# The end of an adaLN and routed-FFN kernel: column steps behind the last product, stores on two queues, and the bias load behind the gathers

## The chip, the cores and the metric

The kernel runs on one core of one Trainium2 chip. A core has five engines that work side by side and are held together by semaphores: TensorE (PE in the profile; its weight loads have their own row, PEld), VectorE (DVE), ScalarE (ACT), GpSimd (POOL) and SyncE (SP). Each engine takes its instructions in the order in which they stand in its queue. Transfers between HBM and on-chip memory are issued from SP, ACT or POOL and carried out by 16 DMA engines that all of these share. The metric is the device time of one execution in microseconds. Lower is better. Three runs of the kernel before took 415.0, 415.74 and 415.83 us, median 415.74.

## What is computed

All numbers are float32. x has 64 batches of 64 rows and 1,024 columns.

```python
W = weights[condition]                       # per batch a 64x64 matrix, chosen by an index 0..15
c = einsum('bct,bcd->bdt', x, W)
logits = c @ gate_w.T + expert_bias          # 4 experts
one_hot = one_hot(argmax(logits))
base  = einsum('bth,oh->bto', c, W_up)       # 1024 x 1024
z     = einsum('nh,erh->ner', c, lora_A)     # 4 experts, rank 8
delta = einsum('ner,ehr->neh', z, lora_B)    # taken for the chosen expert alone
out = x + base + delta
```

So each batch is mixed along its rows by a chosen 64x64 matrix and multiplied by one wide matrix that all batches share.

## The kernel before

The kernel swaps the two products. It first multiplies x by one matrix that holds the gate (4 columns), lora_A (32 columns) and W_up (1,024 columns), 1,060 columns in all; the result is called u. Then it applies the 64x64 matrices to u. Two batches make a **pair** of 128 rows, so there are 32 pairs, and two pairs, called a and b, make a **group**. The matrix is cut in halves along both axes, into blocks B11, B12, B21 and B22 of 512 x 530; each pair's x into two halves of 512 columns (A11 and A12 for pair a, A21 and A22 for pair b).

To keep float32 accuracy, every operand is split into a high part, rounded to fp32r by ScalarE (`ah`, `hB`, `uh` in the profile), and a low part, the rest, taken by VectorE (`al`, `lB`, `ul`). A product is three matmuls: high by high, high by low, low by high. The first two groups take eight block products each (`eight`). All later groups take seven, from sums and differences of blocks (`seven`): `S1` to `S4` of x, and the blocks `T1` to `T4`.

**From u to the output.** The columns of a pair's u are worked off in column steps. `finish(i, j)` is one step: `apply` (three matmuls of the 64x64 matrices, laid out as one 128x128 block `bd`, with `uh`, `uh`, `ul`), `delta` (one matmul that adds the chosen expert's part, from `zt`), and `evict`, which moves the result out of PSUM. The first step of a pair holds the 36 gate and lora columns; `gate` (six small VectorE operations, the first of which, `lg`, adds `bias_sb`) finds the expert and makes `z`, and `turn` transposes it by TensorE and splits it into `zt`. For most pairs `evict` copies to `y`, POOL adds x by an accumulating transfer, and SP stores. For the last pair (`i == NP - 1`, pair b of the last group), and for the last two steps of pair a, x has been loaded into `y` before; VectorE adds, and a store of that step follows at once. The first 480 columns of pair a are stored by themselves.

**The order of work** is written out by hand. `InOrder` wraps the five engines and keeps each one's instructions in the order in which the program makes them. A product runs over four rows `k` of a block, and `hooks` name what is put in after which row. All these calls go through one helper, so they carry line 43 in the profile and are told apart by their tiles.

**The start.** TensorE runs `WARM` small matmuls on a tile of zeros while the first loads come in (`keep_warm`, line 385). Then the first group's products begin with A11 and A21 by B11, row by row. The loads stand on SP's queue in the order B11 row 0, B11 row 1, rest of the first half of x for both pairs, B11 rows 2 and 3, the second half of x (`xx`, one transfer for A12 and A22), B21, B12. After row 0 come the hooks of line 519 on: five more small matmuls, the split of row 1, `make_idx` (a matmul and a VectorE operation that turn the conditions into row indices) and four `load_cond`, gathers of 64x64 matrices that POOL issues by these indices. POOL's queue before them holds constants and, in line 473, the load of the bias, repeated over 128 partitions.

**The end.** In the last group the last wide product, S4 by B22, is made by `product_by_bank`: its 530 columns lie in two PSUM banks, 258 and 272 columns, one worked off after the other. `u_bank(m)` adds the earlier sum `t8` and makes the high part of bank m's u for pair a; `u_bank_low(m)` makes its low part. The column steps of pair b stand between and within the banks, those of pair a behind.

Of the kernel before, what the change touches and what calls it, by code (L numbers as in the profile page):

```python
# [15 lines left out]
P = 128  # L16
# [3 lines left out]
E, R = 4, 8  # L20
# [6 lines left out]

COLS = ((0, 356), (356, 352), (708, 352))
LAST = ((0, 356), (356, NB - 356), (NB, 258), (NB + 258, NB - 258))
WARM = 28  # L30
GATE = (("lg", E), ("mx", 1), ("sc", E), ("m2", 1), ("zm", ER))
HALVES = (slice(0, 64), slice(64, 128))

# [13 lines left out]
def kernel(  # L47
# [147 lines left out]
    def chain():  # L195
        return psum.tile([P, 1024], F32, name="c", tag="c", bufs=3)
# [47 lines left out]
    def u_low(i, n, src):  # L244
        h, lo = us[i]
        vector.tensor_sub(lo[:, n], src, h[:, n].bitcast(F32))
# [5 lines left out]
    def half(hf):  # L252
        return slice(NB * hf, NB * hf + NB)
# [101 lines left out]
    def evict(i, j):  # L355

        s, d = ycols(i, j)
        o = os_.pop((i, j))[:, s]
        if i == NP - 1 or d.start >= FIRST and i == NP - 2:
            vector.tensor_add(ys[i][:, d], o, ys[i][:, d])  # L360
            if d.start == FIRST:
                d = slice(STORED, d.stop)
            sync.dma_start(out[i, :, d], ys[i][:, d])
            return
        if i < NP - 2 and j == 0:
            ys[i] = yp.tile([P, H], F32, name="y", tag="y")
        scalar.copy(ys[i][:, d], o)
        if i == NP - 2 and j == 1:
            n = slice(0, FIRST)
            pool.dma_start(ys[i][:, n], x[i][:, n], accum_op=ALU.add)  # L370
        elif j == 2:
            pool.dma_start(ys[i], x[i], accum_op=ALU.add)
            nc.sync.dma_start(out[i], ys.pop(i))

    def finish(i, j, o=None):
        apply(i, j, o)
        delta(i, j)
        evict(i, j)
# [91 lines left out]
    for e in range(E):  # L470
        pool.memset(rank[:, e : e + 1], float(E - e))
    bias_sb = cpool.tile([P, E], F32, name="bias_sb")
    pool.dma_start(bias_sb, bias.to_broadcast([P, E]))
    b3 = cpool.tile([3 * ER, H], F32R, name="b3")

    PARTS = slice(0, COLS[0][1] - G), slice(COLS[0][1] - G, H)
# [28 lines left out]
    def eight(g):  # L505
        a, b = 2 * g, 2 * g + 1
        h = [[] for _ in range(6 if g == 0 else 8)]

        def at(s, k, fn, *args):
            h[s].append((k, fn, *args))  # L510

        def each(s, k, fn, q, ks, *args):
            for i in ks:
                at(s, k, fn, q, i, *args)

        one, two = (0, 1), (2, 3)
        if g == 0:
            each(0, -1, load_b, "B12", range(KH))
            at(0, 0, keep_warm, 5)
            for n in pieces:  # L520
                at(0, 0, split_b, "B11", 1, n)
            at(0, 0, make_idx)
            for i in range(4):
                at(0, 0, load_cond, i)
            at(0, 0, split_a, g, "A11", STEPS[2])
            each(0, 0, split_b, "B11", (2,))
            at(0, 0, split_a, g, "A21", STEPS[2])
            each(0, 0, split_b, "B11", (3,))
            at(0, 0, split_a, g, "A12")
            each(0, 0, split_b, "B21", (0,))  # L530
            at(0, 1, split_a, g, "A22")
            each(0, 2, split_b, "B21", (1, 2))
            each(0, 3, split_b, "B21", (3,))
            each(1, -1, load_b, "B22", range(KH))
            at(1, 0, load_b3)
            for i in (2, 3):
                at(1, 0, load_half, i, 0)
            each(1, 0, split_b, "B12", (0,))
            each(1, 1, split_b, "B12", (1,))
            each(1, 2, split_b, "B12", two)  # L540
            at(1, 2, split_cond, a)
            at(1, 3, split_cond, b)
            each(1, 3, split_b, "B22", (0,))
            at(2, -1, lambda: u_of(a, 0, c["1"]))
            at(2, 0, load_two, 0)
            at(2, 0, load_two, 1)
            each(2, 0, split_b, "B22", (1,))
            at(2, 2, apply, a, 0)
            at(2, 2, gate, a)
            at(2, 2, lambda: u_of(b, 0, c["2"]))  # L550
            at(2, 3, split_b3, PARTS[0])
            at(3, 1, turn, a)
            for i in (2, 3):
                at(3, 0, load_half, i, 1)
            each(3, 1, split_b, "B22", two)
            at(3, 2, split_a, g + 1, "A11")
            at(3, 3, delta, a, 0)
            at(3, 3, evict, a, 0)
            at(3, 3, split_b3, PARTS[1])
            at(4, 1, apply, b, 0)  # L560
            at(4, 1, gate, b)
            at(4, 2, split_a, g + 1, "A21")
            at(5, -1, lambda: u_of(a, 1, c["3"]))
            at(5, 0, turn, b)
            at(5, 0, sum_t1, one)
            at(5, 0, load_two, 2)
            at(5, 0, load_two, 3)
            at(5, 2, delta, b, 0)
            at(5, 2, evict, b, 0)
            at(5, 2, end_t1, one)  # L570
            at(5, 3, split_a, g + 1, "A12")
            at(5, 3, finish, a, 1)
            order = (
                [("1", "A11", "B11", True), ("2", "A21", "B11", True)],
                [("1", "A12", "B21", False), ("2", "A22", "B21", False)],
                ("3", "A11", "B12", True),
                ("1", "A21", "B12", True),
                ("3", "A12", "B22", False),
                ("1", "A22", "B22", False),
            )  # L580
        else:
            p = a - 1
            at(0, -1, lambda: u_of(p, 1, cs[g - 1]["1"]))
            at(0, 1, finish, p - 1, 2)
            at(0, 1, split_a, g, "A22")
            at(0, 2, make_t1, two)
            at(0, 3, finish, p, 1)
            at(1, 0, finish, p, 2)
            at(1, 1, load_cond, a + 2)
            at(1, 1, load_cond, b + 2)  # L590
            for i in (b + 2, a + 2):
                at(1, 1, load_half, i, 0)
                at(2, 1, load_half, i, 1)
            at(2, 1, make_t2, one)
            at(3, -1, lambda: u_of(a, 1, c["1"]))
            at(3, 2, make_t2, two)
            at(4, -1, lambda: u_of(b, 1, c["2"]))
            at(4, 1, sums, g + 1, "S1")
            at(4, 2, split_cond, a)
            at(4, 2, split_cond, b)  # L600
            at(5, 0, sums, g + 1, "S2")
            at(5, 1, split_a, g + 1, "A11")
            at(5, 2, sums, g + 1, "S3")
            at(6, 0, split_a, g + 1, "S2")
            at(7, -1, lambda: u_of(a, 0, c["3"]))
            at(7, 0, sums, g + 1, "S4")
            order = (
                ("1", "A11", "B12", True),
                ("2", "A21", "B12", True),
                ("1", "A12", "B22", False),  # L610
                ("2", "A22", "B22", False),
                ("3", "A11", "B11", True),
                ("1", "A21", "B11", True),
                ("3", "A12", "B21", False),
                ("1", "A22", "B21", False),
            )
        run(g, order, h, c)
        cs[g] = dict(c)


    def seven(g):
# [123 lines left out]
        if last:  # L745

            z = chain()
            turn(b, z[:, :512])
            u_add(b, c["3"], ts["t7"])
            scalar.copy(us[b][0][:, half(1)], ts["u", b])  # L750
            keep_sum("t8", c["3"], "t6")
            u_low(b, half(1), ts["u", b])
            s = temp("usum")
            places = place(), place()

            def u_bank(m):
                n = LAST_BANKS[m]
                vector.tensor_add(s[:, n], places[m][:, : n.stop - n.start], ts["t8"][:, n])
                scalar.copy(us[a][0][:, NB + n.start : NB + n.stop], s[:, n])

            def u_bank_low(m):
                n = LAST_BANKS[m]
                u_low(a, slice(NB + n.start, NB + n.stop), s[:, n])

            product_by_bank(
                g,
                places,
                "S4",
                "B22",
                [  # L770
                    (3, lambda: finish(b, 0, z[:, 512:])),
                    (3, u_bank, 0),
                    (5, lambda: finish(b, 1, chain()[:, :512])),
                    (5, u_bank_low, 0),
                ],
            )
            sync.dma_start(out[a, :, :STORED], ys[a][:, :STORED])
            u_bank(1)
            finish(b, 2, chain()[:, :512])
            u_bank_low(1)  # L780
            finish(a, 2)
            finish(a, 3)

# [49 lines left out]
```

## Time and profile before

| what | value |
|---|---|
| three runs | 415.0, 415.74, 415.83 us |
| the profiled execution, its own time | 415.6 us |
| its span, first to last instruction | 413.8 us |
| PE busy | 409.4 us, 99% of the span |
| DVE, ACT, POOL busy | 286.2, 185.1, 74.9 us |
| granted TensorE clock | 0.999 of full speed |
| start of the first product | 4.18 us |
| bias load issued on POOL's queue | 4.20 us |
| end of the last matmul | 410.46 us |
| last store issued on SP's queue | 410.96 us |

The profile is of one execution. Its span leaves out 1.8 us of the execution's own time that lie outside the first and last instruction. A row of the timeline gives start, duration, engine, line, operation, the tiles written and read (`out<-in`), their shapes, and in brackets the idle time before it with what ended it. `xN` merges N instructions that follow each other. The ends of matmuls are modelled and overlap the next ones, so it is their starts that are to be compared. In the table of waits a row reads: who waited, for whom, us in total, how often, longest. In the DMA view a queue's row gives packets, megabytes and the share of 16 engines' time in that window; q1 is SP's queue, q10 ACT's, q0 POOL's.

### The profile page before, as it was taken

How to read it: one execution, taken by the hardware profiler on the slowest of the kernel's cores; microseconds unless marked ns; L12 is line 12 of the kernel's file. 1: busy time of each engine (PE TensorE's matmuls, PEld its weight loads, DVE VectorE, ACT ScalarE, POOL GpSimd, SP SyncE). 2: the span in 40 equal slices, each digit the busy share in tenths (PEclk: the TensorE clock that was granted, in tenths of full speed). 3: DMA queues.
4: the chain of work that ended last, by engine and by line, in shares of the span. 5: the costliest groups of instructions: out<-in, count | busy, mean ns of one | idle time of the engine just before them, and what ended most of it. 6: DMA issues, size and time to landing. Idle time of an engine off the chain costs nothing.

```text
span 413.8 us, 8162 instructions
## 1 busy us (share of the span) xinstructions
PE 409.4 (99%) x3193; PEld 407.9 (99%) x3193; DVE 286.2 (69%) x648; ACT 185.1 (45%) x419; POOL 74.9 (18%) x92
## 2 busy tenths in 40 slices
PE   9999999999999999999999999999999999999996
PEld 8999999999999999999999999999999999999996
DVE  5887786866767666676676767666676676766766
ACT  5846744453534445333353534445333343533531
POOL 5205412020020201102020020201102020020000
PEclk9999999999999999999999999999999999999999
DMA  8989974543656435465452556434465442555345
GB/s 266 314 288 229 242 175 87 148 121 98 174 133 169 98 89 144 128 177 125 111 124 95 171 135 174 104 84 139 126 179 135 107 122 93 170 140 149 52 101 178
DMA packets 25830, 60.99 MB, mean 147 GB/s; under 512 B 3328, under 2 KB 5344, under 8 KB 25792
## 3 DMA queue, kind: packets, MB, share of 16 engines
q1 hardware_dynamic: 18544, 41.00, 27.9%
q0 software_dynamic: 6704, 19.21, 27.1%
q8 instruction: 25, 0.41, 0.4%
q10 hardware_dynamic: 544, 0.26, 0.2%
q14 instruction: 13, 0.11, 0.1%
HBM read 43.68 MB, written 16.78 MB: 146 GB/s over the span
## 4 chain that ended last, share of the span: by engine, by line
PE 99%; DVE 0%; issue 0%
PE c L43 82%; PE o L43 17%; DVE y L43 0%; DVE warm L43 0%; DVE one L43 0%
## 5 line engine op out<-in xcount | busy, mean ns | idle before, releaser
L43 PE MATMUL c<-hT,ah 128*128 128x264 f32 x480 | 139.7, 291 | 0.0
L43 PE MATMUL c<-lT,ah 128*128 128x264 f32 x480 | 137.3, 286 | 0.0
L43 PE MATMUL c<-hT,al 128*128 128x264 f32 x480 | 137.1, 286 | 0.0
L43 PE MATMUL c<-hB,ah 128*128 128x264 f32 (+1 forms) x424 | 121.8, 289 | 0.0
L43 PE MATMUL c<-hB,al 128*128 128x264 f32 (+1 forms) x424 | 121.2, 287 | 0.0
L43 PE MATMUL c<-lB,ah 128*128 128x264 f32 (+1 forms) x424 | 119.1, 287 | 0.0
L43 PEld LDWEIGHTS c<-lT,ah 128*128 128x128 f32 x480 | 91.0, 190 | 0.0
L43 PEld LDWEIGHTS c<-hT,ah 128*128 128x128 f32 x480 | 90.9, 189 | 0.0
L43 PEld LDWEIGHTS c<-hT,al 128*128 128x128 f32 x480 | 90.7, 189 | 0.0
L43 POOL DMA_DIRECT2D y<-in_x_dram x31 | 29.7, 957 | 289.6 <-ACT y L43 284.5
L43 PEld LDWEIGHTS c<-hB,ah 128*128 128x128 f32 x424 | 80.8, 190 | 0.3 <-issue 0.3
L43 PEld LDWEIGHTS c<-hB,al 128*128 128x128 f32 x424 | 80.7, 190 | 0.2 <-issue 0.2
L43 PEld LDWEIGHTS c<-lB,ah 128*128 128x128 f32 x424 | 79.6, 190 | 0.1
L43 ACT COPY y<-o 128x352 f32<-128x352 f32 (+1 forms) x91 | 40.1, 443 | 58.2 <-PE o L43 55.1
L43 ACT CAST uh<-usum 128x530 fp32r<-128x530 f32 (+4 forms) x44 | 27.1, 616 | 69.7 <-DVE usum L43 69.7
L43 DVE TENSOR_TENSOR al<-S,ah 128x512 fp32r<-128x512 f32 x56 | 38.5, 688 | 24.1 <-ACT ah L43 24.1
L43 DVE TENSOR_TENSOR al<-xh,ah 128x512 fp32r<-128x512 f32 x46 | 31.7, 690 | 29.9 <-ACT ah L43 29.9
L43 PE MATMUL o<-uh,bd 128*128 128x356 f32 (+2 forms) x186 | 44.8, 322 | 0.0
L43 DVE TENSOR_TENSOR ul<-usum,uh 128x530 fp32r<-128x530 f32 (+4 forms) x44 | 30.1, 683 | 18.7 <-ACT uh L43 18.6
L43 ACT CAST zt<-o 96x128 fp32r<-96x128 f32 x31 | 8.1, 262 | 76.4 <-PE o L43 76.4
L43 POOL DMA_INDIRECT wsel<-in_cw_dram,idx x32 | 34.2, 1070 | 11.9 <-issue 5.2
L43 ACT CAST ah<-S 128x512 fp32r<-128x512 f32 x56 | 34.9, 623 | 1.8 <-DVE S L43 1.4
(88 smaller groups left out, 472.2 us busy)
## 6 DMA issues: line engine op xcount, KB each, us to landing
xh<-in_xt_dram SPq DMA_DIRECT2D x60, 256.0 KB
y<-in_x_dram POOLq DMA_DIRECT2D x30, 512.0 KB, 5.6
out_dram<-y SPq DMA_DIRECT2D x30, 512.0 KB
wraw<-in_w_dram SPq DMA_DIRECT2D x23, 265.0 KB
T<-in_w_dram POOLq DMA_DIRECT2D x8, 265.0 KB, 7.8
xx<-in_xt_dram SPq DMA_DIRECT2D x1, 512.0 KB
wsel<-in_cw_dram,idx POOLq DMA_INDIRECT x32, 5.0
y<-in_x_dram SPq DMA_DIRECT2D x1, 512.0 KB
```

What stands on the lines that cost most here:

```text
L43: return lambda *a, **k: self.tc.keep_in_program_order(fn(*a, **k))
```

## The change

It has four parts. `WARM` goes from 28 to 30, and the small matmuls after the first row from 5 to 1. The bias load moves on POOL's queue from ahead of the gathers to behind them. The last product keeps its two banks, but no column step stands within it: all three of pair b follow behind bank 1, and the VectorE operations are reordered to that, with the low part of b's second half behind the sum of bank 0. The three stores of the last pair are issued by ScalarE, not SP.

```diff
-WARM = 28
+WARM = 30
@@ def evict(i, j, o=None)
             if d.start == FIRST:
                 d = slice(STORED, d.stop)
-            sync.dma_start(out[i, :, d], ys[i][:, d])
+            queue = scalar if i == NP - 1 else sync
+            queue.dma_start(out[i, :, d], ys[i][:, d])
             return
@@ constants
     bias_sb = cpool.tile([P, E], F32, name="bias_sb")
-    pool.dma_start(bias_sb, bias.to_broadcast([P, E]))
@@ def eight(g), g == 0
-            at(0, 0, keep_warm, 5)
+            at(0, 0, keep_warm, 1)
             for n in pieces:
                 at(0, 0, split_b, "B11", 1, n)
             at(0, 0, make_idx)
             for i in range(4):
                 at(0, 0, load_cond, i)
+            at(0, 0, lambda: pool.dma_start(bias_sb, bias.to_broadcast([P, E])))
@@ def seven(g), last group
             keep_sum("t8", c["3"], "t6")
-            u_low(b, half(1), ts["u", b])
@@
                 "S4",
                 "B22",
-                [
-                    (3, lambda: finish(b, 0, z[:, 512:])),
-                    (3, u_bank, 0),
-                    (5, lambda: finish(b, 1, chain()[:, :512])),
-                    (5, u_bank_low, 0),
-                ],
+                [(3, u_bank, 0), (3, lambda: u_low(b, half(1), ts["u", b]))],
             )
+            u_bank(1)
+            u_bank_low(0)
+            finish(b, 0, z[:, 512:])
+            u_bank_low(1)
+            finish(b, 1, chain()[:, :512])
             sync.dma_start(out[a, :, :STORED], ys[a][:, :STORED])
-            u_bank(1)
             finish(b, 2, chain()[:, :512])
-            u_bank_low(1)
             finish(a, 2)
             finish(a, 3)
```

## The prediction

> **What bounds the kernel now.** I read the page first: busy shares and the chain that ended last.
>
> ```profile
> PE 409.4 (99%) x3193; PEld 407.9 (99%) x3193; DVE 286.2 (69%) x648; ACT 185.1 (45%) x419; POOL 74.9 (18%) x92
> PE 99%; DVE 0%; issue 0%
> ```
>
> TensorE is never off the chain until the last eviction, so time can only be won where TensorE stands still, does work that is not needed, or after it has ended. I took the step from each matmul's start to the next in the timeline and compared it with the usual step of its shape (0.123 us for 264 columns, 0.126 for 272, 0.16 for 352). Between 13.5 and 409.4 us just one place is late (62.1 us, 0.2 us, behind TensorE's own earlier results). So three places are left: the start up to 13.5 us, the last two column steps, and the time after the last matmul. TensorE at the start, then what feeds it:
>
> ```profile
> 7.01 0.47 PE L43 MATMUL o<-warm 128*128 128x128 bf16 x5
> 7.41 0.18 PE L43 MATMUL o<-condf,batch 2*128 2x32 bf16 x1
> 7.53 0.39 PE L43 MATMUL c<-hB,ah 128*128 128x264 f32 x1
> ...
> 12.59 0.51 PE L43 MATMUL c<-lB,ah 128*128 128x264 f32 x2
> 12.94 0.28 PE L43 MATMUL c<-hB,ah 128*128 128x264 f32 x1
> 13.19 0.39 PE L43 MATMUL c<-hB,al 128*128 128x264 f32 x1
> ```
> ```profile
> 10.34 0.62 ACT L43 CAST ah<-xx 128x512 fp32r<-128x512 f32 x1 [1.36 <-DMA xx<-in_xt_dram]
> 11.16 0.64 ACT L43 CAST hB<-wraw 128x530 fp32r<-128x530 f32 x1 [0.19 <-issue]
> 11.70 0.61 ACT L43 CAST ah<-xx 128x512 fp32r<-128x512 f32 x1
> ```
> ```profile
> 11.82 0.71 DVE L43 TENSOR_TENSOR lB<-wraw,hB 128x530 fp32r<-128x530 f32 x1
> 12.45 0.69 DVE L43 TENSOR_TENSOR al<-xx,ah 128x512 fp32r<-128x512 f32 x1
> ```
>
> The low part of B21's row 0 ends at 12.53 and TensorE's `lB` matmul starts at 12.59; the low part of A22 ends at 13.14 and TensorE's `al` matmul starts at 13.19. Two waits, and behind each a weight load that nothing hides. By the starts (12.441, 12.591, 12.817, 12.941, 13.192, 13.420) the steps are 0.150, 0.226, 0.251 and 0.228 against about 0.124: 0.36 us lost. Both chains begin at 10.34, when ScalarE had waited 1.36 us for x's second half. Why it lands so late is in the DMA view of 9.10 to 10.25 us:
>
> ```profile
> q1 hardware_dynamic: 204, 0.38, 92.7%
> q0 software_dynamic: 5, 0.00, 9.3%
> ```
>
> Five packets with no bytes to speak of took 9.3% of 16 engines for 1.15 us, 1.7 us. By the packet records two 128-byte packets of POOL's queue took 0.84 us each (9.12 to 9.96, 9.36 to 10.20); the only transfer on that queue by then, apart from one that landed at 5.4, is the bias, issued at 4.20. The increments that x's transfer sends show most engines done from 8.53 to 8.84 and the last at 10.32, right after 10.20. Two engines already trail (the transfer before: 7.66 for most, 7.91 and 8.19 for two). The bias sits on these.
>
> The end:
>
> ```profile
> 409.17 0.28 PE L43 MATMUL o<-b,zt 96*128 96x258 f32 x1
> 409.42 0.52 PE L43 MATMUL o<-uh,bd 128*128 128x272 f32 x2
> 409.94 0.39 PE L43 MATMUL o<-ul,bd 128*128 128x272 f32 x1
> 410.17 0.29 PE L43 MATMUL o<-b,zt 96*128 96x272 f32 x1
> ```
> ```profile
> PEld o L43 <- DVE ul L43: 0.2, 1, 0.2
> PEld o L43 <- ACT uh L43: 0.2, 1, 0.2
> ```
>
> The last column step of batch pair a waits for its own u: TensorE ends at 410.46, VectorE evicts from 410.49 to 410.94, SP issues the last store at 410.96, it has landed at 412.74 (the semaphore that SP waits for), and closing waits and barrier end the span at 413.8.
>
> **What the Trainium skill says.** "DMA: Bandwidth & Descriptors", section "Why a DMA increments its semaphore by 16 and not by 1": engines finish independently and only the full count means landed; so one slow engine holds a whole transfer, which the 8.84 against 10.32 shows. Same page, "Queues, rings and completion order": an engine takes turns between its queues by packets; that puts a slow bias packet in front of x's, and the records agree. Same page, "Issuing engines are not separate DMA queues": a second issuing engine saves the issue time alone; SP's issue here took 0.33 us. "TensorE: Matmul & The Clock Gate", section "The HAM clock gate": full clock comes after some 3.4 us of activity, in a free-running window. The trace: matmul steps of 0.22 us until 7.01, then 0.12.
>
> **The change, part by part.**
>
> *Warm-up, 28 to 30.* Two more at 0.107 us each move TensorE's free point from 3.95 to 4.165. The first product starts at 4.176, held by its data (VectorE's `ah` ends at 4.03), the second at 4.53 by `al`. Cost 0, at most 0.1.
>
> *Fillers, 5 to 1.* The filler starts are 7.009, 7.092, 7.148, 7.204, 7.260, and the index product follows at 7.412. Four fewer take away 0.25 us. Their successors' data is there: `hB` of row 1 by 6.82, `lB` by 7.32, needed about 0.5 us after the new start of 7.28. Later operands have 0.3 us or more in hand until B21's row 0. By itself this only makes the waits at 12.59 and 13.19 longer: worth 0.
>
> *Bias behind the gathers.* x's second half should then land at about 9.5 (10.32 less 0.84; the same result as 8.95, where I put most engines' end, plus the old 0.53 us lag). ScalarE is free at 8.98, so everything from 10.34 on comes up to 0.8 us earlier. With TensorE 0.25 us early, `lB` is wanted at 12.33 instead of 12.57 and `al` of A22 at 12.70; they would be ready at about 11.7 and 12.3. Both waits go: 0.36, and the fillers' 0.25 is kept. 0.61 together; 0.5 us of earlier landing is enough. If the gathers' first packets meet the same delay instead, B21's rows 1 to 3 come as late as today, when they are first used more than a microsecond after landing. Behind the gathers the bias is issued at about 13.1; the old one needed 6.0 us from issue to its last packet, so it lands at about 19.1. Its first reader, VectorE's `lg`, now starts at 21.25, then 20.65: 1.5 us of cover. POOL has nothing behind it until 33.1, and the gathers, whose indices come 0.25 us earlier, no longer stand behind it.
>
> *The end.* The same matmuls run in another order. Bank 0 starts at 403.82 as before, bank 1 now at 405.35, pair b's three column steps from 406.88 on, pair a's at 408.81, the place they have now. Before, the last `uh`/`ul` came 0.1 to 0.3 us late. Now the bank's sum starts when bank 1's last matmul has ended (407.04): VectorE `usum` 407.14 to 407.57, ScalarE `uh` to 408.02, wanted at 409.29. VectorE's queue, by the step of each shape in the rows (530 columns 0.62, 352 0.44, 320 0.40, 258 and 272 0.36): sum of bank 0 at 406.17, low part of b 406.52, sum of bank 1 407.14, low part of bank 0 407.50, then evict 407.85, low part of bank 1 408.25 to 408.68 (wanted at 409.54), evictions 408.59, 409.03, 409.49. VectorE is full but not late, so TensorE's waits go: 409.29 plus four matmuls, end at 409.96 instead of 410.46, last eviction from 410.0. Gain 0.50.
>
> *Stores of pair b by ScalarE.* ScalarE's last copy ends at 408.02, so it is free. SP's last issue depends on the eviction alone, both before and after (0.33 us of issue, 0.7 apart). Worth 0 itself; without it SP would have b's third store, ready at 409.56, in the last 0.9 us. The stores now bunch: 1,024 KB issued from 408.36 to 410.47, against 407.36 to 410.96. At some 390 GB/s (77 to 83 KB per 0.2 us in the packets while busy) the last bytes come at about 411.9, where an undisturbed last store would end at 411.8. Minus 0.1. In the changed program TensorE's bank 1 waits for ScalarE's eviction of 402.72 to 403.15 and SP's store for the loads of y, both long done.
>
> Sum: 0.61 + 0.50 - 0.10 = 1.0 us. The profiled execution took 415.6, with a span of 413.8: span 412.8, time 414.6. The median of the runs is 0.14 above the profiled one, so 414.7.
>
> **Rivals.** (1) *The bias was not what held x*: the long packets only sat on engines that are slow anyway. Then the start gives 0 and the end 0.4: 415.3. For it: the two engines trail before the bias. Against: their lag grows from 0.5 to about 1.4 us just there. (2) *The end gives nothing*: VectorE, with no more than 0.1 us to spare, falls behind, or the bunched stores queue for 0.4 us more. Then 0.6: 415.1. (3) *Slower*: the bias comes too late. Behind `lg` on VectorE stand the gate's five operations, b's low part, b3's split and `zt`, and TensorE's transpose at 23.26 needs `z`, ready at 22.74. With TensorE 0.61 us earlier, `lg` may start at 21.1; a later landing stops TensorE one for one. At 22.1 the 1.0 us gained is spent, and landing at 23.1, 10 us after issue, gives 416.7. The four gathers needed 5.2 to 6.3 us. (4) *The clock window*: full clock came at 7.0 here; a phase with it earlier lets the products before 7 us run faster, by up to 0.4 us now that no wait takes it back: 414.3; a later one costs as much.
>
> **How the numbers follow.** The forecast has 0.56, rival 1 0.16, rival 2 0.12, rival 3 0.08, the early clock 0.08. Time 414.7; its own range is 414.3 to 415.1. For 8 in 10 I go from 414.0 (early clock) to 415.6 (rivals 1 and 2), leaving out the slow case and the edges. A measurement of this kernel tells some 0.2%, 0.83 us, from no change, so faster means below 414.9: most of the forecast, the early clock and a little of rival 2, 0.64. Within: rival 1, the rest of rival 2 and the forecast's edge, 0.28. Slower: 0.08.
>
> **What would show it.** Right: no packet of 0.8 us near 9 us, ScalarE's `ah` from x's second half at about 9.5, TensorE's steps even from 7.3 to 13.5 and B21's first matmul at 11.83 instead of 12.08; at the end no wait of TensorE for `uh` or `ul`, and its last matmul 0.45 to 0.55 us after the 258-column step's last. Wrong: `ah` still at 10.3; `lg` waiting for a DMA near 20.7; a last eviction that starts later than 0.1 us after TensorE's end; more than 1.9 us from the last store's issue to its landing.

## The result, and the profile after

| | us |
|---|---|
| kernel before, median of 22 runs | 415.54 (414.5 to 416.18) |
| changed kernel, median of 22 runs | 414.85 (414.2 to 415.71) |
| ratio, with its 95% interval | 0.9985 (0.9979 to 0.9992) |
| changed kernel, the profiled execution | 415.4, span 413.6 |

The changed kernel is 0.62 us faster by the ratio (0.33 to 0.87). That is real but small: less than the 0.83 us that the prediction took as the least that can be told from no change. The forecast was 414.7.

The page of the changed kernel, busy shares and the chain that ended last:

```profile
PE 408.5 (99%) x3191; PEld 407.7 (99%) x3191; DVE 285.6 (69%) x648; ACT 185.0 (45%) x419; POOL 75.0 (18%) x92
PE 97%; DMA 1%; issue 0%; POOL 0%; DVE 0%; POOLq 0%
```

TensorE is 0.9 us less busy, and yet this execution is only 0.2 us shorter than the profiled one of before. A DMA has come into the chain: the small transfer of the conditions, on which the index product at 7.26 us waits. TensorE at the start, changed kernel:

```profile
6.88 0.23 PE L43 MATMUL o<-warm 128*128 128x128 bf16 x1
7.26 0.17 PE L43 MATMUL o<-condf,batch 2*128 2x32 bf16 x1
7.37 0.39 PE L43 MATMUL c<-hB,ah 128*128 128x264 f32 x1
...
9.36 0.28 PE L43 MATMUL c<-hB,al 128*128 128x266 f32 x1
9.60 0.52 PE L43 MATMUL c<-lB,ah 128*128 128x264 f32 x2
...
12.16 0.28 PE L43 MATMUL c<-hB,ah 128*128 128x264 f32 x1
...
13.66 0.29 PE L43 MATMUL c<-hB,ah 128*128 128x264 f32 x1
```

The four fillers are gone, but 0.38 us pass before the index product, and a step of 0.24 stands at 9.36. B21's first matmul, at 12.08 before, is now at 12.16; the waits behind it (12.59, 12.94 and 13.19 before) are gone, and the second row of B21 starts at 13.66 for 13.91. ScalarE, and the DMA view of 9.10 to 10.25 us:

```profile
10.20 0.62 ACT L43 CAST ah<-xx 128x512 fp32r<-128x512 f32 x1 [0.55 <-issue]
10.89 0.64 ACT L43 CAST hB<-wraw 128x530 fp32r<-128x530 f32 x1
11.44 0.61 ACT L43 CAST ah<-xx 128x512 fp32r<-128x512 f32 x1
```
```profile
q1 hardware_dynamic: 244, 0.46, 104.1%
```

POOL's queue (q0) had 9.3% of the engines there and now has no row at all; SP's queue moves 244 packets in place of 204 (a share over 100% means that packets overlap in the record). Still x's second half is cast at 10.20, not at the 9.5 forecast. In this execution three packets of SP's own queue took 1.22, 0.77 and 0.53 us at 3.70, 5.44 and 6.27 us, and the increments of the transfers show one last engine trailing from then on: B11's row 1 is in at 5.34 for most engines and at 6.74 for the last, and the next three transfers trail in the same way. Of x's second half itself only 11 of the 16 increments are in the trace, the last at 9.08, so that this engine held it until 10.2 as well is likely but not shown.

The end, TensorE of the changed kernel:

```profile
408.89 0.28 PE L43 MATMUL o<-b,zt 96*128 96x258 f32 x1
409.01 0.42 PE L43 MATMUL o<-uh,bd 128*128 128x272 f32 x2
409.27 0.29 PE L43 MATMUL o<-ul,bd 128*128 128x272 f32 x1
409.39 0.29 PE L43 MATMUL o<-b,zt 96*128 96x272 f32 x1
```

The last two column steps run through without a wait, and the two rows of TensorE waiting for `ul` and `uh` are gone from the table of waits. From the first matmul of the last wide product (403.559 us; 403.816 before) to the last matmul of all it is 5.83 us, before 6.35: 0.52 won. But from that same matmul to the end of the span it is 10.03 us, before 10.00. All of the 0.52 is lost again after the last matmul. The last store is issued 0.80 us after the last matmul in both kernels; its issue to its last packet takes 1.36 us before and 1.90 after. Busy time by window, three microseconds each, at the same distance from the last wide product's first matmul; first before, then after (the last two columns are the DMA engines' busy share and GB/s):

```profile
409.25:412.25 3.00, 1.20 (x6) 0.59 (x4) 1.41 (x4) 0.12 (x1) 0.00 (x0) 1.00 0.75 265
```
```profile
409.00:412.00 3.00, 0.68 (x6) 0.46 (x4) 1.09 (x3) 0.00 (x0) 0.00 (x0) 1.00 0.99 349
```

The 16 DMA engines are full for three microseconds. Two theories follow. **A**: the start gives the whole gain; the end gives none, because the six last stores, 1,024 KB, now stand before the DMA engines together. **B**: the end gives its share too and the start only 0.25, as this one profile has it.

### The profile page after: what moved, and what is told of

Read it like the earlier page. It is cut to its first block, busy times and chain, and to the rows that moved or that the text cites. A ratio compares the mean times of both kernels' runs of the same rounds, so it can differ in the third digit from the quotient of the medians.

```text
span 413.6 us, 8160 instructions
## 1 busy us (share of the span) xinstructions
PE 408.5 (99%) x3191; PEld 407.7 (99%) x3191; DVE 285.6 (69%) x648; ACT 185.0 (45%) x419; POOL 75.0 (18%) x92
## 4 chain that ended last, share of the span: by engine, by line
PE 97%; DMA 1%; issue 0%; POOL 0%; DVE 0%; POOLq 0%
PE c L43 81%; PE o L43 16%; DMA cond_sb<-in_cond_dram 1%; DVE y L43 0%; POOL which L43 0%; POOL condf L43 0%; POOLq L43 0%; POOLq L818 0%
## 5 line engine op out<-in xcount | busy, mean ns | idle before, releaser
L43 POOL DMA_INDIRECT wsel<-in_cw_dram,idx x32 | 34.9, 1089 | 10.6 <-issue 5.2
```

Of the source, the lines that this page charges most:

```text
L43: return lambda *a, **k: self.tc.keep_in_program_order(fn(*a, **k))
```

## The experiments

All are compared by three marks: S, the first matmul of B21's second row; M, the first matmul of the last wide product; and the end of the span. From S to M it is 389.90 to 389.92 us in every one of the 14 profiles, so a kernel's span is its S, plus 389.9, plus what follows M. The table anticipates all runs.

| kernel | bias | end | S, us | M to the last matmul | M to the end | median | ratio to before (95%) |
|---|---|---|---|---|---|---|---|
| before | ahead | before | 13.91 | 6.35 | 10.00 | 415.5 to 415.8 | |
| changed | behind | changed | 13.66 | 5.83 | 10.03 | 414.85 | 0.9985 (0.9979 to 0.9992) |
| changed, once more | behind | changed | 13.23 | 5.84 | 10.03 | 414.85 | 0.9985 (0.9976 to 0.9993) |
| e1_start | behind | before | 13.02 | 6.34 | 9.98 | 414.70 | 0.9983 (0.9976 to 0.9989) |
| e2_tail | ahead | reordered, SP alone | 13.77 | 5.82 | 10.34 | 415.74 | 1.0003 (0.9994 to 1.0012) |
| e3_tail_queue | ahead | changed | 13.94 | 5.84 | 10.03 | 415.29 | 1.0000 (0.9989 to 1.0011) |
| e4_queue | ahead | before, b's stores by ScalarE | 14.19 | 6.39 | 10.03 | 415.44 | 1.0000 (0.9991 to 1.0009) |
| e5_bias | behind | before | 12.64 | 6.36 | 10.10 | 415.02 | 0.9984 (0.9974 to 0.9994) |
| e6_fill | ahead | before | 13.62 | 6.36 | 10.01 | 415.40 | 0.9992 (0.9983 to 1.0001) |
| e7_early | behind | changed, early store | 12.94 | 5.84 | 9.70 | 414.54 | 0.9970 (0.9958 to 0.9982) |
| e7_again | behind | changed, early store | 12.43 | 5.84 | 9.69 | 414.48 | 0.9979 (0.9972 to 0.9986) |
| e8_no_b | behind | changed, no stores of b | 13.09 | 5.82 | 9.73 | 414.40 | 0.9968 (0.9956 to 0.9980) |
| e9_old_end | behind | before, early store | 13.15 | 6.35 | 9.92 | 414.75 | 0.9981 (0.9974 to 0.9988) |
| e10_end_early | ahead | changed, early store | 13.41 | 5.83 | 9.70 | 414.96 | 0.9993 (0.9984 to 1.0002) |

The median of the kernel before was 415.5 to 415.8 from one set of runs to the next, so ratios are what to compare.

### The change in halves

`e1_start` is the kernel before with the start of the change: 30 and 1 fillers, and the bias behind the gathers.

```diff
-WARM = 28
+WARM = 30
-    pool.dma_start(bias_sb, bias.to_broadcast([P, E]))
-            at(0, 0, keep_warm, 5)
+            at(0, 0, keep_warm, 1)
+            at(0, 0, lambda: pool.dma_start(bias_sb, bias.to_broadcast([P, E])))
```

> The kernel before with the two changes at the start alone (bias load behind the gathers; small matmuls 30 and 1). Theory A (the start gives all of the gain, the end gives none because its stores queue in the DMA engines): 0.6 us faster than before, and the time from the first matmul of the last product to the end of the span stays at 9.97 us. Theory B (the end gives its share, the start gives 0.25 us as the one profile shows): 0.25 us faster.

`e2_tail` is the kernel before with the undivided product and the new order behind it, all stores still on SP. `e3_tail_queue` adds the stores of pair b by ScalarE, which makes it the whole end of the change. `e4_queue` has only these stores by ScalarE, in the old order.

```diff
                 "B22",
-                [
-                    (3, lambda: finish(b, 0, z[:, 512:])),
-                    (3, u_bank, 0),
-                    (5, lambda: finish(b, 1, chain()[:, :512])),
-                    (5, u_bank_low, 0),
-                ],
+                [(3, u_bank, 0), (3, lambda: u_low(b, half(1), ts["u", b]))],
@@ ... and the order of the calls behind it as in the change
```
```diff
-            sync.dma_start(out[i, :, d], ys[i][:, d])
+            queue = scalar if i == NP - 1 else sync
+            queue.dma_start(out[i, :, d], ys[i][:, d])
```

> The kernel before with the reordered end alone, all stores still on SP. TensorE's waits go in both theories: from the first to the last matmul start of the end 5.83 us instead of 6.35. Theory A: the 0.50 us are more than lost in the stores, which stand one behind the other on SP and then in the engines; first matmul of the last product to the end of the span 10.2 us against 9.97, the kernel 0.1 to 0.3 us slower. Theory B, and the sum that I had predicted (queue worth nothing): 0.4 us faster.

> The kernel before with the reordered end and pair b's stores issued by ScalarE. Theory A: no gain, within 0.1 us of before; the end takes 10.0 us, the last store needs 2.3 us from issue to landing. Theory B: 0.4 us faster, end 9.5 to 9.6 us.

> The kernel before with pair b's stores issued by ScalarE and nothing else. If ScalarE's queue itself lands its stores late (rival to theory A's crowding), b's stores need 2.2 us from issue to landing here too; if crowding is the cause they need 1.8 us as from SP, and the last store still lands 1.78 us after its issue. Time within 0.1 us of before either way.

Measured: the start alone gives 0.71 us (0.46 to 1.00 by its ratio), as much as the whole change. The end alone, `e3_tail_queue`, gives 0.0 with an interval of 0.46 to either side, which by itself would still allow the 0.4 of theory B. The marks decide it: in all three profiles with the changed end (the changed kernel twice, and this one) it is 10.03 us from M to the end, and with the end of before it is 9.98 to 10.10 in four. In `e3_tail_queue` 5.84 us lead to the last matmul, 0.51 won, and none of it reaches the end. Theory A stands.

`e2_tail` prices the second queue. It loses more after M than expected (10.34 us for 10.2), and timed it is not told from the kernel before: 0.12 us slower by its ratio, with an interval from 0.25 faster to 0.50 slower. SP's stores in it, and VectorE's last evictions:

```profile
408.24 3.10 SPq L43 DMA_DIRECT2D out_dram<-y  x6
409.34 0.91 DVE L43 TENSOR_TENSOR y<-o,y 128x258 f32<-128x258 f32 x2
```

VectorE is done at 410.25, but SP issues its last store at 410.93, because its issues follow each other by 0.42 to 0.54 us. With two queues the last issue came 0.03 us after the last eviction. So ScalarE saves 0.64 us of issue. Of that only 0.31 is kept (10.34 to 10.03), since the earlier stores meet more traffic: 1.56 us from the last issue to the last packet in `e2_tail`, 1.87 in `e3_tail_queue`. In the old order, where SP isn't pressed, the queue is worth nothing (`e4_queue`: 10.03 for 10.00). Nor does ScalarE's queue itself land its stores late: the first of pair b's stores takes 1.82 us from issue to landing in `e4_queue`, and 1.78 from SP in `e1_start`.

### Which part of the start

`e5_bias` moves the bias alone and keeps the fillers; `e6_fill` changes the fillers alone and leaves the bias ahead.

```diff
-    pool.dma_start(bias_sb, bias.to_broadcast([P, E]))
+            at(0, 0, lambda: pool.dma_start(bias_sb, bias.to_broadcast([P, E])))
```
```diff
-WARM = 28
+WARM = 30
-            at(0, 0, keep_warm, 5)
+            at(0, 0, keep_warm, 1)
```

> Only the bias's load is moved behind the gathers; the 28 and 5 fillers and the whole end stay as before. Theory A (x's second half and what lands after it bound the start of the kernel before): `ah` of x's second half starts at 9.5-9.7 us instead of 10.3, the waits in B21's first row are gone, and most of the gain of the start comes with it: -0.4 to -0.6 us, 414.9-415.1. Theory B (the fillers that TensorE no longer runs are the gain): -0.1 or less, 415.4.

> Only the fillers change (30 ahead, 1 between the first rows); the bias's load stays ahead of x's halves and the end stays as before. Theory A: the 0.2 us that TensorE saves is given back in the wait for x's second half: 0 to -0.1 us, 415.4-415.5, B21's second row starts no sooner than in the kernel before (13.7-14.2 us). Theory B: -0.25 us or more, 415.2.

The bias alone gives 0.67 us (0.25 to 1.08), as much as the whole start within these intervals. The fillers alone measure 0.33 us faster, with an interval from 0.71 faster to 0.04 slower: not told from nothing, and not from theory B's 0.25 either. S is 13.62, a little sooner than theory A expected. Its profile shows where the fillers' time goes, first ScalarE, then the DMA view of 8 to 10.6 us, then TensorE:

```profile
8.85 0.62 ACT L43 CAST ah<-xx 128x512 fp32r<-128x512 f32 x1 [0.57 <-DMA xx<-in_xt_dram]
10.86 0.63 ACT L43 CAST hB<-wraw 128x530 fp32r<-128x530 f32 x1 [1.39 <-DMA wraw<-in_w_dram]
```
```profile
q1 hardware_dynamic: 378, 0.71, 78.4%
q0 software_dynamic: 32, 0.00, 20.6%
```
```profile
11.54 0.39 PE L43 MATMUL c<-hB,ah 128*128 128x264 f32 x1 [0.53 <-ACT hB L43]
```

Here x's second half slips through at 8.85, but the next load, B21's row 0, meets the bias: ScalarE waits 1.39 us for it and TensorE stands still until 11.54. POOL's 32 packets take a fifth of all engines' time while the megabytes that they move round to 0.00. In this profile eight 128-byte packets of POOL's queue took 0.69 to 1.17 us each, between 8.1 and 10.1 us. In `e10_end_early`, the one profile with the bias ahead in which no packet of POOL's queue took over 0.5 us there, S is 13.41, the earliest of its kind and sooner than expected. With the bias behind the gathers such a packet is in none of the eight profiles. Over all profiles S lies at 13.41 to 14.19 with the bias ahead (six, mean 13.81) and at 12.43 to 13.66 with it behind (eight, mean 13.02): 0.79 us apart. The profile of the changed kernel, with its trailing engine, is the worst of the eight.

### Is it the crowd of stores?

`e7_early` takes the largest store, 480 columns of pair a, out of the crowd. The first 494 columns of that pair's x are loaded ahead into a buffer of their own, GpSimd adds them in place of the accumulating DMA, and the store follows at once. `e8_no_b` leaves the three stores of pair b out, so half of the last pair's output is missing.

```diff
+        if i == NP - 2:
+            xa = raw["xa"] = xp.tile([P, KH, P], F32, name="xh", tag="xh").rearrange(
+                "p a b -> p (a b)"
+            )[:, :FIRST]
+            nc.sync.dma_start(xa, x[i][:, :FIRST])
@@ def evict(i, j, o=None)
-            pool.dma_start(ys[i][:, n], x[i][:, n], accum_op=ALU.add)
+            pool.tensor_add(ys[i][:, n], ys[i][:, n], raw["xa"])
+            sync.dma_start(out[i, :, :STORED], ys[i][:, :STORED])
@@ last group
-            sync.dma_start(out[a, :, :STORED], ys[a][:, :STORED])
```

> The changed kernel, with the 480-column store of pair a taken out of the last rush: pair a's first 494 columns of x are loaded ahead into a buffer of their own, GpSimd adds them to the evicted columns in SBUF in place of the accumulating DMA, and the store of 480 columns follows at once, near 405-406 us instead of 408.3. Theory A (the stores fill the DMA engines from 409 to 412 us): 240 KB less in the rush lets the last store land 1.4-1.5 us after its issue for 1.9, first matmul of the last wide product to the end of the span 9.5-9.6 us for 10.0: 414.3-414.5. Theory B (a fixed delay of the last store, whatever else moves): 10.0 us still, 414.85.

> The changed kernel with the three stores of pair b's rows left out, so that half of the last pair's output is not written; all arithmetic stays. It prices the crowding by itself. Theory A: nothing is in the way of the last store, it ends 1.35-1.4 us after its issue (to the last packet) instead of 1.9, first matmul of the last wide product to the end of the span 9.45-9.5 us for 10.0, 414.3. Theory B: no change, 414.85.

Both end 0.30 to 0.33 us sooner after M, with TensorE unchanged at 5.82 to 5.84. Theory A holds in kind. The size is smaller than expected, 0.4 to 0.55, for two reasons. In `e7_early` the last store still takes 1.62 us to its last packet, for 1.36 in a calm end: 784 KB remain. In `e8_no_b` the last packet is as quick as in a calm end (1.38), but 1.73 us pass from it to the end of the span, for 1.51 in the changed kernel; why stays open.

### What the end is worth once there is room

`after_again` is the changed kernel once more, `e7_again` the one with the early store, `e9_old_end` is `e1_start` with the early store, `e10_end_early` is `e7_early` with the start of before (28 and 5 fillers, bias ahead).

> The changed kernel once more, beside the two that follow on the same chip. Both theories: 414.85 us, 0.6-0.7 below the kernel before; first matmul of the last wide product to the end of the span 10.0 us. If TensorE's pace doubles at 5 us here, as in most profiles, and not at 6.75, B21's second row starts near 13.0 us and not at 13.66.

> The kernel with the 480-column store sent ahead, once more, timed beside the changed kernel on the same chip. Theory A (crowding): 0.3 us below the changed kernel, 9.70 us from the last wide product's first matmul to the end. Theory B (the first comparison was drift of the kernel before): equal to the changed kernel within 0.1 us.

> The start of the changed kernel with the end of the kernel before (divided product, all stores on SP), and the 480-column store sent ahead. Theory A: in the old end the last store already goes out into nearly idle DMA engines (1.36 us to its last packet), so that there is nothing to win from room: 414.7, equal to the start alone, 9.95-10.0 us from the last wide product's first matmul to the end; the undivided product is then worth 0.3 us, but only with the early store. Theory B (the early store is worth 0.3 us by itself): 414.4.

> The start of the kernel before with the end of the changed kernel and the 480-column store sent ahead. Theory A: the end's share shows by itself once the stores have room: -0.3 us against the kernel before, 415.2-415.3, 9.7 us from the last wide product's first matmul to the end, B21's second row at 13.6-14.2 us. Theory B: equal to the kernel before.

Timed side by side, the early store is 0.37 us below the changed kernel by the medians (414.48 for 414.85; by the means of 17 and 14 runs 0.42, 95% 0.22 to 0.62). GpSimd and SP in `e7_again`, and its three microseconds at the same distance from M as above:

```profile
402.88 1.25 POOL L43 TENSOR_TENSOR y<-y,xh 128x494 f32<-128x494 f32 x1 [4.83 <-ACT y L43]
```
```profile
404.15 5.13 SPq L43 DMA_DIRECT2D out_dram<-y  x3
```
```profile
407.76:410.76 3.00, 0.69 (x6) 0.46 (x4) 1.10 (x3) 0.00 (x0) 0.00 (x0) 1.00 0.77 268
```

The addition takes 1.25 us where the accumulating transfer took 3.9 from issue to landing, the store of 480 columns is issued 1.83 us after M and not 4.74, and the engines are busy for 0.77 of the window and not for 0.99. With the old end the same early store buys next to nothing: `e9_old_end` has 9.92 us after M, `e1_start` 9.98, and 414.75 us is no better than 414.70. With the same start and the same early store, the changed end (`e7_again`) is faster than the old one (`e9_old_end`) by 0.23 us in the means of 17 and 21 runs (95% 0.04 to 0.42). So it isn't the early store by itself. The changed end, undivided product and two queues together, has 0.2 to 0.3 us in it (9.69 and 9.70 after M, for 9.92 and 10.00), and it needs room in the DMA engines to give them out. `e10_end_early` agrees by its span (9.70 for 10.00); timed it is 0.29 us faster by its ratio, with an interval from 0.66 faster to 0.08 slower, so not told from no change.

The early store on top of the change thus beats both kernels: 0.9979 (0.9972 to 0.9986) of the kernel before in the larger set of runs, `e7_again`.

## Why the prediction was right, and where it was not

The forecast of 414.7 us was a sum of 1.0 us: 0.61 from the start and a net 0.4 from the end. The runs show 0.71 from the start and nothing from the end. That 414.85 still lies close to the forecast is in part luck: the start's extra 0.1 and a kernel before whose median was 0.2 us lower in this set (415.54 for 415.74) cover most of the 0.4 that is missing.

**Bias behind the gathers (0.61 with the fillers): right.** The start alone measured 0.71, and the second profile of the changed kernel shows nearly the forecast steps; ScalarE, then TensorE:

```profile
9.05 0.62 ACT L43 CAST ah<-xx 128x512 fp32r<-128x512 f32 x1 [0.57 <-DMA xx<-in_xt_dram]
```
```profile
6.95 0.23 PE L43 MATMUL o<-warm 128*128 128x128 bf16 x1
7.11 0.19 PE L43 MATMUL o<-condf,batch 2*128 2x32 bf16 x1
7.23 0.39 PE L43 MATMUL c<-hB,ah 128*128 128x264 f32 x1
...
11.77 0.28 PE L43 MATMUL c<-hB,ah 128*128 128x264 f32 x1
13.23 0.29 PE L43 MATMUL c<-hB,ah 128*128 128x264 f32 x1
```

Row 1 at 7.23 (forecast 7.28), B21 at 11.77 (forecast 11.83), S 0.68 before that of the kernel before; x's second half is cast at 9.05, sooner than the 9.5 forecast. Rival 1, that the bias only sat on slow engines, falls: `e5_bias`. One reading of the prediction is weaker than it sounds: of the increments of x's transfer the trace of before holds 7 of 16, so "most engines" done by 8.84 is six of seven.

**The fillers' 0.25 kept: right for one pace of TensorE, nothing in the mean.** The split into 0.36 and 0.25 rests on a profile in which TensorE ran at about half its pace until 7.0 us. In 10 of the 14 profiles the steps shrink from 0.22 to 0.12 between 4.6 and 5.3 us. Then TensorE is done with B11's first row near 6.1 us and catches up with the loads of the later ones. `e1_start`:

```profile
6.12 0.23 PE L43 MATMUL o<-warm 128*128 128x128 bf16 x1
6.28 0.18 PE L43 MATMUL o<-condf,batch 2*128 2x32 bf16 x1
6.60 0.39 PE L43 MATMUL c<-hB,ah 128*128 128x264 f32 x1
...
8.74 0.28 PE L43 MATMUL c<-hB,al 128*128 128x266 f32 x1
8.94 0.51 PE L43 MATMUL c<-lB,ah 128*128 128x264 f32 x2
```

Row 1 comes at 6.60, after a step of 0.32, and row 2's `lB` is waited for at 8.74. With five fillers at the same pace (`e5_bias`) row 1 comes at 6.64, no later row is waited for, and S is 12.64 for 13.02. Timed, the two are alike (0.9984 and 0.9983): what the fillers give is below what these runs can tell. The quick pace is rival 4's early window. By these profiles it is the ordinary case, not one of 0.08. With the bias ahead it is taken back: `e2_tail` and `e3_tail_queue`, at the quick pace from 5.1 and 5.2 us, have one step of 0.7 us near 11 us for the usual 0.12, and their S is 13.77 and 13.94. With the bias ahead the mean of S is 13.78 in the five profiles of quick pace and 13.91 in the one of late pace; with it behind 12.82 in five and 13.35 in three. So in these profiles the start profits from the pace once it doesn't wait behind the bias.

**The end on TensorE (0.50): right,** 0.52 measured, with no wait for `uh` or `ul`.

**Stores bunched (0.10): the step that failed.** That they bunch was right. The prediction put the last bytes 0.1 us after an undisturbed store's. Measured is 412.08 against 410.187 + 1.36 = 411.55, 0.53 us. 1,024 KB at the forecast's 390 GB/s, a rate read off single slices of 0.2 us, are 2.69 us, which left 0.85 us between the first issue (408.36) and the first byte; measured is 0.87, so that wasn't it. The rate was: the packets of these stores have 1,088 to 1,920 bytes. By their medians (56, 79, 60 and 52 ns for rows of 1,280, 1,920, 1,408 and 1,088 bytes; 8, 8, 16 and 16 of them for each engine) the 1,024 KB need 2.87 us, not 2.69: 0.18 of the miss. Another 0.20 is what the engines need beyond that sum (409.01 to 412.08 is 3.07 us), for a reason that the runs don't show, and 0.06 is the shorter stretch from first to last issue. The warning sign was named, more than 1.9 us from the last store's issue to its landing; it was 2.33. This is the second half of rival 2, with 0.4 us of queueing at the price that it gave, and 415.1; the start, 0.1 better than its sum, makes up part of the way from there to 414.85, and the rest is within the interval.

**ScalarE's stores, "worth 0 itself": wrong in the new order.** There SP alone would issue the last store 0.64 us late, and 0.31 us of that reach the end.

**The bias late (rival 3): closer than forecast.** In the first profile the load is issued at 13.71 and lands at 20.01, for 13.1 and 19.1 in the prediction. In the second profile of the changed kernel it lands at 20.7, and VectorE waits for it:

```profile
20.74 0.16 DVE L43 TENSOR_TENSOR lg<-o,bias_sb 128x4 f32<-128x4 f32 x1 [1.65 <-DMA bias_sb<-in_bias_dram]
```

In the profiles where the bias is early, `lg` starts 7.34 us after S, when TensorE has its other input ready; here that would be 20.57, so the bias is late by 0.17 us only, and TensorE loses nothing: S to M is 389.90 us as everywhere. The cover of 1.5 us in the prediction was in truth 1.0 us in one profile and less than none in the other.

## What to carry to other kernels

A saving behind the last matmul is only worth what the stores let through: sum the bytes of the last stores over the rate of their own row size, from the first one's data on, and compare it with the last issue plus a calm store's time; if the sum is longer, send bytes ahead before making the compute shorter. A tiny load by POOL's queue can hold a large transfer that shares the engines with it, so whatever isn't wanted early belongs behind what is. And where start-up depends on TensorE's pace, one profile is one draw: split the program at marks and look at several.

## What the runs showed of the hardware

- One to eight of the bias's sixteen 128-byte packets on POOL's queue took 0.55 to 1.17 us each while the engines were full of SP's loads, in five of the six profiles with the bias ahead. In the sixth, `e10_end_early`, the median of such a packet is 15 ns and the longest 0.32 us. SP's 2,120-byte packets took 87 ns in the median beside them. What makes a packet slow isn't shown.
- Stores to HBM by row size, medians: 52 ns a packet for 1,088 bytes (48 in the kernel before), 60 for 1,408, 79 for 1,920, 160 for 4,096, that is 335, 375, 389 and 410 GB/s over 16 engines. The Trainium skill's page "DMA: Bandwidth & Descriptors", section "Why small descriptors are slow (HBM only)", names a fixed overhead per packet. The trace agrees, and shows it well above the 256 bytes of that section's example: from 1,920 to 4,096 bytes the time grows by 0.037 ns a byte, which leaves an estimated 7 to 8 ns a packet that don't depend on its size.
- TensorE's pace about doubled between 4.6 and 7.1 us, in executions of kernels whose first 28 small matmuls and first products are the same. The page "TensorE: Matmul & The Clock Gate", section "The HAM clock gate", says that the window is free-running and gives a spread of 0.5 us to either side; here it is some 1.2. The column of the granted clock doesn't show it. `e1_start` and the changed kernel from 5 to 6 us, with 10 and 7 matmuls and 1.00 in both:

```profile
5.00:6.00 1.00, 1.00 (x10) 1.00 (x9) 0.64 (x4) 0.16 (x1) 0.20 (x1) 1.00 0.94 322
```
```profile
5.00:6.00 1.00, 1.00 (x7) 1.00 (x6) 0.67 (x4) 0.19 (x1) 0.00 (x0) 1.00 1.08 368
```
